# Softmax sums of an attention: ones-matmul on TensorE, or a trip through DRAM

## The chip, the cores and the metric

One core of a Trainium2 chip runs the whole kernel in one launch. TensorE multiplies matrices, VectorE and ScalarE work on SBUF and PSUM, GpSimd does little here, and SyncE (SP) issues nearly all DMAs. Times are device microseconds. The time before is the median of three runs; the profile is of one further execution with its own time.

## The reference

The input is x of shape (4, 256, 64, 64) in fp32: four images of 256 channels and 4096 pixels. Four layers follow, each of the form x = x + layer(group_norm(x)). The change lies in the first, whose middle is an attention over all pixels:

```python
xs = relu(group_norm(conv3x3(x, smooth_w) + smooth_b))
f = einsum('bnc,bcm->bnm', theta_x, phi_x)      # 4096 x 4096 logits per image, 128 channels
attn = softmax(f, axis=-1)
y = einsum('bnm,bmc->bnc', attn, g_x)
w_y = group_norm(conv1x1(y, w_w, w_b))
return w_y * 0.1 + xs
```

The other three layers are a linear attention, a convolution with generated filters and a mix of expert matrices. All is fp32.

## The kernel before, in words

**The attention.** `attend(b)` is a generator over one image. It takes the 4096 queries in eight blocks of 512 (`NQ = 8`), and each block in 16 steps of 256 keys (`NM = 16`). Keys stand on partitions, queries along the free dimension. In a step, `logits(i + 1)` makes the next step's two tiles pf of 128 keys by 512 queries (L984) and ScalarE exponentiates them into pr (L985). Then two matmuls add g times pr to the block's output py in PSUM (L1040), and VectorE adds pr to tot, a tile of 128 x 1024 running sums (L124, a helper's line). There is no maximum to subtract.

**The end of a block.** After step 15, tot holds for each query sums that are still spread over 128 partitions and two halves. `ended` finishes them: VectorE adds the two halves into inv (L992) and leaves a check sum in guard; a matmul with a matrix of ones (L996) sums over the partitions and leaves the total of each query on every partition (pss); VectorE inverts it (L1013, 128 x 512 elements); yt = py * inv; ScalarE runs through inv once for the second check sum (L1017); two matmuls with ww give ps_wy (L1021), copied to wt (L1022). wt gets statistics (L1025) and goes to DRAM as wy_d. In the last image also the residual's block xc is loaded from xs_d and its statistics are taken (L1051, L963). `ended` is itself a generator, kept in `todo`: it goes on by one `yield` at the end of each step of the next block, after that step's addition to tot.

**The order of the work.** The order on every engine is that of the program, written out by hand (`manual_schedule`). While image b attends, a `Chain` puts other work between its steps: the rest of the previous image's layers (`tail`) and the convolution of the next image (`convolve`, `convolve_second`, with filter tiles u loaded ahead at L478). `run` advances the attention by a step per unit of the chain. An engine executes its list in order, and each instruction waits for semaphores. So an instruction that waits holds up all behind it on its engine. SP too works through its DMAs in one order: a DMA that waits for another's landing, or for VectorE, holds up the next ones' issue.

**Buffers.** `k4` is a pool of nine tiles of 128 x 1024 (pr, tot, wt, xc and the chain's tiles), `k2` one of five tiles of 128 x 512 (yt, parts of products, res, the tiles of the output). PSUM has eight banks, one pool. inv has one buffer.

Of the kernel before, what the change touches and what calls it, by code (L numbers as in the profile page):

```python
# [8 lines left out]
F32 = mybir.dt.float32  # L9
AF = mybir.ActivationFunctionType  # L10
ALU = mybir.AluOpType
AX = mybir.AxisListType

P = 128
NH = 2
HW = 64
N = HW * HW
CH = 1024
# [6 lines left out]
NQ = N // 512  # L25
# [68 lines left out]
def conv_preact_fast(ctx: ExitStack, tc: tile.TileContext, guard, x, wc, wtpg, ww, wqkv, wout, w1cat, wd2,  # L94
# [3 lines left out]
    nc = tc.nc  # L98
    B = x.shape[0]

    cp = ctx.enter_context(tc.tile_pool(name="const", bufs=1))
    wk = ctx.enter_context(tc.tile_pool(name="work", bufs=1))
    sp = ctx.enter_context(tc.tile_pool(name="small", bufs=2))
    pp = ctx.enter_context(tc.tile_pool(name="ps", bufs=1, space=bass.MemoryType.PSUM))

    def k4(name):
        return wk.tile([P, CH], F32, tag="k4", name=name, bufs=9)
# [1 line left out]
    pool4 = k4  # L109

    def k2(name):
        return wk.tile([P, 512], F32, tag="k2", name=name, bufs=5)

    def filter_tile(name):
        return wk.tile([P, NH, NH * P], F32, tag="u", name=name, bufs=3)
# [1 line left out]
    def junk():  # L117
        return wk.tile([P, 512], F32, tag="junk", name="junk")

    def bank(name):  # L120
        return pp.tile([P, 512], F32, tag="bank", name=name, bufs=8)

    def tt(o, a, b, op):
        nc.vector.tensor_tensor(o, a, b, op)  # L124
# [33 lines left out]
    def resident(name, src):  # L158
        t = cp.tile(list(src.shape), F32, name=name)
        nc.sync.dma_start(out=t, in_=src)  # L160
        return t
# [8 lines left out]
    ww_s = resident("ww_s", ww)  # L170
# [50 lines left out]
    def scale_weights(w):  # L221


        nc.vector.tensor_scalar(bo_s, bo_s, 1.0 / HEADS, None, ALU.mult)

        nc.vector.tensor_scalar(gains, vec_s[:, V_GN:V_GN + 2, :], float(NH * P) ** 0.5, None, ALU.mult)
        for h in range(NH):
            nc.vector.tensor_scalar(wqkv_s[:, h, :], wqkv_s[:, h, :], gains[:, 0, h:h + 1], None, ALU.mult)
        yield 1.5

        ps = bank("ps_wn")
        for h in range(NH):
            sq = k2("wsq")
            nc.scalar.activation(sq[:, 0:2 * HID], wqkv_s[:, h, 0:2 * HID], AF.Square)
            yield 1
            nc.tensor.matmul(ps[:, 0:2 * HID], ones, sq[:, 0:2 * HID], start=(h == 0), stop=(h == NH - 1))
        wmax = sp.tile([P, 1], F32, name="wmax", bufs=1)
        nc.vector.tensor_reduce(wmax, ps[:, 0:2 * HID], AX.X, ALU.max)
        for side in range(2):
            nc.vector.tensor_scalar(guard[:, side, B * NQ:B * NQ + 1], wmax, GUARD_MAX[side] / NORM2_MAX, None, ALU.mult)  # L240
# [157 lines left out]
    xs_d = tc.dram_tile([B, NH, P, N], F32, name="xs_d")  # L398
    wy_d = tc.dram_tile([B, NH, P, N], F32, name="wy_d")
# [536 lines left out]
    NM = N // CH * 4  # L936

    wy_stats = {}


    res_st = cp.tile([P, NH, NQ, 6], F32, name="res_st")
# [7 lines left out]
    def residual_known():  # L949
        nc.vector.tensor_scalar(factors[:, 0, :], vec_s[:, V_G2W, :], 0.1, None, ALU.mult)  # L950
        nc.vector.tensor_scalar(factors[:, 1, :], vec_s[:, V_G2B, :], 0.1, None, ALU.mult)
        res_mv.append(sp.tile([P, NH, 2], F32, name="rmv", bufs=1))
        for h in range(NH):
            nc.vector.bn_aggr(res_mv[0][:, h, :], res_st[:, h, :, :].rearrange("p c s -> p (c s)"))
        tt(res_shift, res_mv[0][:, :, 0], factors[:, 1, :], ALU.add)

    def attend(b):

        probs, todo = {}, []
        st = wy_stats[b] = sp.tile([P, NH, 8, 6], F32, name="wy_st")  # L960

        def multiply(q, h, wt, xc):
            nc.vector.scalar_tensor_tensor(xc[:, h, :], wt[:, h, :], pivot_in[:, h:h + 1], xc[:, h, :], ALU.add, ALU.mult,  # L963
                                           accum_out=joint[:, h, q:q + 1])

        def with_residual(q, wt, xc):

            if q == 0:
                mv = sp.tile([P, NH, 2], F32, name="mv")
                for h in range(NH):  # L970
                    nc.vector.bn_aggr(mv[:, h, :], st[:, h, 0, :])
                nc.vector.tensor_scalar(pivot_in, mv[:, :, 0], -1.0, None, ALU.mult)
            if q < NQ - 1:
                for h in range(NH):
                    multiply(q, h, wt, xc)
            else:
                last_block.extend(lambda h=h: multiply(q, h, wt, xc) for h in range(NH))

        def logits(i):
            q, m = divmod(i, NM)  # L980
            pr = k4("pr")
            for s in range(2):
                pf = bank("pf")
                nc.tensor.matmul(pf, phi[:, bass.ts(2 * m + s, P)], theta[:, bass.ts(q, 512)], start=True, stop=True)  # L984
                nc.scalar.activation(pr[:, bass.ts(s, 512)], pf, AF.Exp)  # L985
            probs[i] = pr

        def ended(q, py, tot, xc):

            at = b * NQ + q  # L990
            inv = wk.tile([P, 512], F32, tag="inv", name="inv")
            nc.vector.scalar_tensor_tensor(inv, tot[:, 0:512], 1.0, tot[:, 512:CH], ALU.mult, ALU.add,  # L992
                                           accum_out=guard[:, 0, at:at + 1])
            yield
            pss = bank("pss")
            nc.tensor.matmul(pss, ones, inv, start=True, stop=True)  # L996
            wt = k4("wt").rearrange("p (h n) -> p h n", h=NH)
            if at == B * NQ - 1:

                yt = k2("yt")  # L1000
                nc.scalar.copy(yt, py)
                banks = [bank("ps_wy") for _ in range(NH)]
                for h in range(NH):
                    nc.tensor.matmul(banks[h], ww_s[:, bass.ts(h, P)], yt, start=True, stop=True)
                yield
                nc.vector.reciprocal(inv, pss)
                for h in range(NH):
                    tt(wt[:, h, :], banks[h], inv, ALU.mult)
                nc.scalar.activation(junk(), inv, AF.Copy, accum_out=guard[:, 1, at:at + 1])
                yield  # L1010
            else:
                yield
                nc.vector.reciprocal(inv, pss)  # L1013
                yt = k2("yt")
                tt(yt, py, inv, ALU.mult)
                yield
                nc.scalar.activation(junk(), inv, AF.Copy, accum_out=guard[:, 1, at:at + 1])  # L1017

                for h in range(NH):
                    ps = bank("ps_wy")  # L1020
                    nc.tensor.matmul(ps, ww_s[:, bass.ts(h, P)], yt, start=True, stop=True)  # L1021
                    nc.scalar.copy(wt[:, h, :], ps)  # L1022
            yield
            for h in range(NH):
                nc.vector.bn_stats(st[:, h, q, :], wt[:, h, :])  # L1025
            nc.sync.dma_start(out=wy_d[b].rearrange("h p n -> p h n")[:, :, bass.ts(q, 512)], in_=wt)
            if b == B - 1:
                with_residual(q, wt, xc)

        xc = None  # L1030
        logits(0)
        for i in range(NQ * NM):
            q, m = divmod(i, NM)
            if m == 0:
                py = bank("py")
                tot = k4("tot")
            if i + 1 < NQ * NM:
                logits(i + 1)
            for s in range(2):
                nc.tensor.matmul(py, g[:, bass.ts(2 * m + s, P)], probs[i][:, bass.ts(s, 512)],  # L1040
                                 start=(m == 0 and s == 0), stop=(m == NM - 1 and s == 1))
            if m == 1:
                tt(tot, probs[i - 1], probs[i], ALU.add)
            elif m > 1:
                tt(tot, tot, probs[i], ALU.add)
            if b == B - 1 and m == 9:
                xc = k4("xc").rearrange("p (h n) -> p h n", h=NH)
                nc.sync.dma_start(out=xc, in_=xs_d[b].rearrange("h p n -> p h n")[:, :, bass.ts(q, 512)])
            if b == B - 1 and m in (12, 14):
                h = m // 2 - 6  # L1050
                nc.vector.bn_stats(res_st[:, h, q, :], xc[:, h, :])  # L1051
                if q == NQ - 1 and h == NH - 1:
                    residual_known()
            for t in todo:
                next(t, None)
            if m == NM - 1:
                todo = [ended(q, py, tot, xc)]
                next(todo[0])
            yield i + 1 < NQ * NM
        for t in todo:  # L1060
            for _ in t:
                yield
# [1284 lines left out]
```

## Time and profile before

| | |
|---|---|
| median of three runs | 3085.98 us (3084.27 to 3086.03) |
| the profiled execution | 3084.23 us |
| its span | 3082.4 us |
| TensorE busy, instructions | 3000.3 us (97%), 8606 |
| VectorE busy | 2128.5 us (69%) |
| ScalarE busy | 1162.0 us (38%) |
| DMA, mean rate | 178.45 MB, 58 GB/s |
| TensorE's granted clock | 0.993 |

A row of a profile gives the line and engine, what is written from what, the shape and the count; then the busy time, the mean of one in ns, and the idle time of the engine just before, with the one that ended it. PE is matmul, PEld the load of a matmul's weights, which overlaps the matmuls; DVE is VectorE, ACT ScalarE, SPq SyncE's queue. Ends of matmuls are modelled, so their starts tell more than their durations. The attention of image 0 runs from 185 to 757 us, of image 1 to 1501, of image 2 to 2242 and of image 3 to about 2820; the last image's remaining layers follow alone.

### The profile page before, as it was taken

Reading aid. Unit: us, or ns where it says so; the run is one execution under the profiler, and the core shown is the slowest. Engines: PE = TensorE matmul, PEld = TensorE weight load, DVE = VectorE, ACT = ScalarE, POOL = GpSimd, SP = SyncE. Lnnn points to the kernel's source line nnn. Section 1 sums busy time; section 2 is a strip of 40 time slices with the busy share of each in tenths; the row PEclk is TensorE's granted clock in tenths of the full one; section 3 lists DMA queues with packets and bytes.
Section 4 is the critical chain, followed back from the end, with each engine's and each line's share of the span. In section 5 each row is a group of like instructions: output and inputs, shape, how many; then the busy total and the mean of one; then the engine's idle time right before and its main releaser. Section 6 shows DMA issues by size and latency. Waiting matters only on the chain.

```text
span 3082.4 us, 24468 instructions
## 1 busy us (share of the span) xinstructions
PE 3000.3 (97%) x8606; PEld 1483.7 (48%) x8606; DVE 2128.5 (69%) x2780; ACT 1162.0 (38%) x2155; POOL 132.1 (4%) x178
## 2 busy tenths in 40 slices
PE   6899999999999999999999999999999999999998
PEld 3454555445554444444565444444546544444643
DVE  8747777853547996777536797678563569876485
ACT  2334333353555332223364532222436453334621
POOL 0100000000010000000011000000001100000100
PEclk9999999999999999999999999999999999999999
DMA  5233111122100023113300102311420000022021
GB/s 219 84 101 137 34 48 32 34 52 73 57 11 28 14 75 122 39 40 66 116 1 11 35 7 82 123 45 38 96 82 14 18 28 28 14 82 89 8 69 66
DMA packets 61089, 178.45 MB, mean 58 GB/s; under 512 B 6560, under 2 KB 16544, under 8 KB 56736
## 3 DMA queue, kind: packets, MB, share of 16 engines
q1 hardware_dynamic: 56928, 160.04, 15.1%
q0 software_dynamic: 4032, 16.78, 2.9%
q8 instruction: 70, 1.15, 0.2%
q14 instruction: 59, 0.48, 0.1%
HBM read 115.45 MB, written 78.12 MB: 63 GB/s over the span
## 4 chain that ended last, share of the span: by engine, by line
PE 77%; DVE 16%; issue 5%; ACT 1%; POOL 0%; DMA 0%; POOLq 0%; DVEq 0%; ACTq 0%
PE pf L984 22%; PE py L1040 22%; PE ps_qkv L1201 5%; PE ps_conv L512 4%; PE ps_tp L926 4%; DVE dw L127 4%; PE ps_ex L1660 4%; DVE tot L124 3%; PE ps_pw L1460 3%; PE ps_conv L584 2%; PE ps_g L931 2%; PE ps_wy L1021 2%; PE ps_o L1287 1%; PE ps_dw L1505 1%; DVE big L127 1%
## 5 line engine op out<-in xcount | busy, mean ns | idle before, releaser
L985 ACT ACTIVATE pr<-pf 128x512 f32<-128x512 f32 x1024 | 603.9, 597 | 1195.4 <-PE pf L984 1147.9
L984 PE MATMUL pf<-tpg 128*128 128x512 f32 x2048 | 968.9, 595 | 2.9 <-ACT pr L985 2.9
L1040 PE MATMUL py<-pr,tpg 128*128 128x512 f32 x2048 | 962.3, 592 | 2.5 <-ACT pr L985 2.3
L124 DVE TENSOR_TENSOR tot<-tot,pr 128x1024 f32<-128x1024 f32 x448 | 546.3, 1219 | 174.1 <-ACT pr L985 172.5
L1040 PEld LDWEIGHTS py<-pr,tpg 128*128 128x128 f32 x2048 | 388.6, 190 | 494.6 <-issue 477.6
L984 PEld LDWEIGHTS pf<-tpg 128*128 128x128 f32 x2048 | 382.0, 190 | 438.4 <-issue 412.6
L127 DVE SCALAR_TENSOR_TENSOR dw<-xp,dk,dw 128x1008 f32<-128x1008 f32 x208 | 263.0, 1268 | 9.9 <-ACT dw L1452 7.0
L512 PE MATMUL ps_conv<-v,u 128*128 128x512 f32 x384 | 171.0, 593 | 3.6 <-DVE v L124 3.6
L1201 PE MATMUL ps_qkv<-wqkv_s,xg 128*128 128x384 f32 x384 | 129.9, 487 | 0.0
L124 DVE TENSOR_TENSOR tpg<-ps_g,bg_s 128x512 f32<-128x512 f32 x32 | 22.1, 692 | 145.2 <-PE ps_g L931 145.2
L926 PE MATMUL ps_tp<-big,wtpg_s 128*128 128x512 f32 x256 | 117.7, 603 | 3.0 <-ACT big L684 3.0
L512 PEld LDWEIGHTS ps_conv<-v,u 128*128 128x128 f32 x384 | 72.6, 190 | 96.5 <-issue 89.8
L217 POOL TENSOR_TENSOR rstd<-rstd,half 128x2 f32<-128x2 f32 x24 | 17.6, 731 | 2342.1 <-DVE rstd L365 2225.2
L1013 DVE RECIPROCAL inv<-pss 128x512 f32<-128x512 f32 x31 | 103.9, 3352 | 5.5 <-PE pss L996 5.5
L1460 PE MATMUL ps_pw<-dw,pk 128*128 128x512 f32 x224 | 101.3, 592 | 0.0
L1201 PEld LDWEIGHTS ps_qkv<-wqkv_s,xg 128*128 128x128 f32 x384 | 72.2, 190 | 53.6 <-issue 9.8
L1220 DVE TENSOR_REDUCE qs<-qk 128x16 f32<-128x512 f32 x24 | 16.5, 686 | 117.4 <-ACT qk L1214 117.4
L927 ACT ACTIVATE tpg<-ps_tp,btp_s 128x512 f32<-128x512 f32 x64 | 43.8, 687 | 119.2 <-PE ps_tp L926 119.2
L926 PEld LDWEIGHTS ps_tp<-big,wtpg_s 128*128 128x128 f32 x256 | 47.8, 194 | 54.9 <-issue 50.4
L1289 ACT ACTIVATE junk<-ps_o 128x256 f32<-128x256 f32 x128 | 49.2, 385 | 63.9 <-PE ps_o L1287 56.3
L1214 ACT ACTIVATE qk<-ps_qkv,rinv 128x256 f32<-128x256 f32 x96 | 45.6, 475 | 72.4 <-PE ps_qkv L1201 60.0
L124 DVE TENSOR_TENSOR v<-ra 128x1024 f32<-128x1024 f32 x58 | 69.5, 1220 | 0.4
(369 smaller groups left out, 3132.7 us busy)
## 6 DMA issues: line engine op xcount, KB each, us to landing
xp<-in_x_dram SPq DMA_DIRECT2D x16, 1024.0 KB, 6.3
wy_d<-wt SPq DMA_DIRECT2D x32, 512.0 KB, 3.0
wy<-wy_d SPq DMA_DIRECT2D x32, 512.0 KB, 4.9
out_dram<-res SPq DMA_DIRECT2D x64, 256.0 KB, 2.0
xs_d<-big POOLq DMA_DIRECT2D x24, 512.0 KB, 11.1
u<-filters SPq DMA_DIRECT2D x48, 256.0 KB, 2.5
xs<-xs_d SPq DMA_DIRECT2D x24, 512.0 KB, 6.1
u<-rows_d SPq DMA_DIRECT2D x36, 256.0 KB, 3.1
```

The costliest lines, as they stand in the source:

```text
L124: nc.vector.tensor_tensor(o, a, b, op)
L127: nc.vector.scalar_tensor_tensor(o, a, s, b, op0, op1)
L512: nc.tensor.matmul(ps[oh], u(oh, h), v[:, bass.ts(h, 512)], start=(h == 0), stop=(h == NH - 1))
L584: nc.tensor.matmul(ps[:, bass.ts(oh, IY * IX)], u[i][:, h, bass.ts(oh, P)], v[:, i, bass.ts(h, IY * IX)], start=(h == 0), stop=(h == NH - 1))
L926: nc.tensor.matmul(ps, wtpg_s[:, h, k, :], big[:, h, cols], start=(h == 0), stop=(h == NH - 1))
L984: nc.tensor.matmul(pf, phi[:, bass.ts(2 * m + s, P)], theta[:, bass.ts(q, 512)], start=True, stop=True)
L985: nc.scalar.activation(pr[:, bass.ts(s, 512)], pf, AF.Exp)
L1013: nc.vector.reciprocal(inv, pss)
L1040: nc.tensor.matmul(py, g[:, bass.ts(2 * m + s, P)], probs[i][:, bass.ts(s, 512)], start=(m == 0 and s == 0), stop=(m == NM - 1 and s == 1))
L1201: nc.tensor.matmul(ps[:, 0:3 * HID], xg[:, h, bass.ts(j, P)], wqkv_s[:, h, :], start=(h == 0), stop=(h == NH - 1))
L1460: nc.tensor.matmul(ps, pk[:, h * NH * P + oh * P:h * NH * P + (oh + 1) * P], dw[h][:, bass.ts(s, 512)], start=(h == 0), stop=(h == NH - 1))
L1660: nc.tensor.matmul(ps, wm[h][:, bass.ts(oh, P)], big[:, h, bass.ts(c, 512)], start=(h == 0), stop=(h == NH - 1))
```

## The change

For the first seven blocks of each image, 28 of 32, `ended_by_dram` replaces `ended`; the eighth block goes as before. py is copied to SBUF at once. The halves' sums inv (128 partitions x 512 queries) are stored to DRAM, and loaded back so that partition r holds, for four queries 4r to 4r + 3, the 128 parts of each: 128 x 4 floats along the free dimension, in pieces of four. VectorE sums over the parts, inverts 128 x 4 values, and they are stored (2 KB) and loaded again with every partition getting all 512. Then yq = yq * inv, the two ww matmuls, and the rest. Each DMA stands some `yield`s, that is steps of the next block, ahead of what uses it. The residual's block xc of the last image is loaded and measured inside `ended_by_dram` for these blocks. k2 gets four tiles in place of five, and a tile yq is new.

```diff
-        return wk.tile([P, 512], F32, tag="k2", name=name, bufs=5)
+        return wk.tile([P, 512], F32, tag="k2", name=name, bufs=4)
...
+    sum_d = tc.dram_tile([B * NQ, P, 512], F32, name="sum_d")
+    rec_d = tc.dram_tile([B * NQ, 512], F32, name="rec_d")
...
+        def residual_block(q):
+            t = k4("xc").rearrange("p (h n) -> p h n", h=NH)
+            nc.sync.dma_start(out=t, in_=xs_d[b].rearrange("h p n -> p h n")[:, :, bass.ts(q, 512)])
+            return t
...
+        def projected(q, wt, xc):
+            for h in range(NH):
+                nc.vector.bn_stats(st[:, h, q, :], wt[:, h, :])
+            nc.sync.dma_start(out=wy_d[b].rearrange("h p n -> p h n")[:, :, bass.ts(q, 512)], in_=wt)
+            if b == B - 1:
+                with_residual(q, wt, xc)
+
+        def ended_by_dram(q, py, tot):
+            at = b * NQ + q
+            inv = wk.tile([P, 512], F32, tag="inv", name="inv")
+            nc.vector.scalar_tensor_tensor(inv, tot[:, 0:512], 1.0, tot[:, 512:CH], ALU.mult, ALU.add,
+                                           accum_out=guard[:, 0, at:at + 1])
+            yt = wk.tile([P, 512], F32, tag="yq", name="yq")
+            nc.scalar.copy(yt, py)
+            nc.sync.dma_start(out=sum_d[at], in_=inv)
+            yield
+            yield
+            nc.sync.dma_start(out=inv.rearrange("r (p k) -> r p k", k=4), in_=sum_d[at].rearrange("p (r k) -> r p k", k=4))
+            yield
+            yield
+            yield
+            r = sp.tile([P, 4], F32, name="r_inv", bufs=1)
+            nc.vector.tensor_reduce(r, inv.rearrange("r (p k) -> r k p", k=4), AX.X, ALU.add)
+            nc.vector.reciprocal(r, r)
+            nc.vector.tensor_reduce(guard[:, 1, at:at + 1], r, AX.X, ALU.add)
+            nc.sync.dma_start(out=rec_d[at].rearrange("(r k) -> r k", k=4), in_=r)
+            xc = residual_block(q) if b == B - 1 else None
+            yield
+            yield
+            nc.sync.dma_start(out=inv, in_=rec_d[at].partition_broadcast(P))
+            yield
+            yield
+            tt(yt, yt, inv, ALU.mult)
+            yield
+            wt = k4("wt").rearrange("p (h n) -> p h n", h=NH)
+            for h in range(NH):
+                ps = bank("ps_wy")
+                nc.tensor.matmul(ps, ww_s[:, bass.ts(h, P)], yt, start=True, stop=True)
+                nc.scalar.copy(wt[:, h, :], ps)
+            if b == B - 1:
+                for h in range(NH):
+                    residual_stats(q, h, xc)
+            yield
+            projected(q, wt, xc)
...
-            if b == B - 1 and m == 9:
...
+            if b == B - 1 and q == NQ - 1 and m == 9:
+                xc = residual_block(q)
...
-                todo = [ended(q, py, tot, xc)]
+                todo = [ended_by_dram(q, py, tot) if q < NQ - 1 else ended(q, py, tot, xc)]
```

## The prediction

> **What bounds the kernel now.** I read the page's busy times first, then the chain, then single instructions at a block's end, then the Vector engine's order and the DMA queues there.
>
> The busy times of the page:
>
> ```profile
> span 3082.4 us, 24468 instructions
> ...
> PE 3000.3 (97%) x8606; PEld 1483.7 (48%) x8606; DVE 2128.5 (69%) x2780; ACT 1162.0 (38%) x2155; POOL 132.1 (4%) x178
> ```
>
> TensorE is busy 97% of the span, but its ends are modelled, so that alone proves little. The chain that ended last agrees:
>
> ```profile
> PE 77%; DVE 16%; issue 5%; ACT 1%; POOL 0%; DMA 0%; POOLq 0%; DVEq 0%; ACTq 0%
> ```
>
> Three quarters of the end time is matmuls that follow one another; DMA is nothing. Now the timeline at the end of image 0's first query block (start, duration, engine, line):
>
> ```profile
> 245.40 0.19 PEld L996 LDWEIGHTS pss<-inv,ones 128*128 128x128 f32 x1 [0.24 <-issue]
> 245.82 1.02 PE L996 MATMUL pss<-inv,ones 128*128 128x512 f32 x2
> 245.82 0.19 PEld L996 LDWEIGHTS pss<-inv,ones 128*128 128x128 f32 x1 [0.24 <-issue]
> 246.25 0.19 PEld L984 LDWEIGHTS pf<-tpg 128*128 128x128 f32 x1 [0.24 <-issue]
> 246.88 3.36 DVE L1013 RECIPROCAL inv<-pss 128x512 f32<-128x512 f32 x1 [0.68 <-PE pss L996]
> ```
>
> The weight loads stand 0.43 us apart: that is what one fp32 instruction of 512 columns costs the stream, not the 0.59 us of its row. One matmul in the code is two of these, 0.86 us. The sum over 128 partitions fits in the same rhythm: it costs 0.86 us per block and nothing waits around it. Since the starts leave hardly any gap in the attention stages, any 0.43 us taken out of TensorE there is time.
>
> The tile view of the sums, minimum/median/maximum in ns:
>
> ```profile
> L996 PE MATMUL pss<-inv,ones x64: 592/592/1061, 245.8 to 2818.2; 128*128 128x512 f32 x64
> L1013 DVE RECIPROCAL inv<-pss x31: 3342/3351/3358, 246.9 to 2766.7; 128x512 f32<-128x512 f32 x31
> ```
>
> 64 instructions are 32 blocks of two; 28 blocks change.
>
> [...] The load that regroups the sums has pieces of four floats, 16 bytes, so 128 x 128 = 16384 of them, 1024 on each of 16 DMA engines. No DMA of the kernel before is like it. [...]
>
> **The change part by part**, for one block.
>
> TensorE: minus one ones-matmul, 2 x 0.43 = 0.86 us. The two ps_wy matmuls only move from the second to the ninth step after the block. 28 x 0.86 = 24.0 us less.
>
> VectorE: minus 3.35 (reciprocal) and 0.69 (yt from PSUM). Plus the reduction to four sums: the nearest row is TENSOR_REDUCE 128x16<-128x512 at 0.69; [...] I take 0.69. Plus a reciprocal and a sum of four elements, 0.16 each by the small rows (L1629, L1625), plus yq times inverse, 0.69. Net 4.04 - 1.70 = 2.3 us less, 65 us in all, on an engine 69% busy: hidden by TensorE, worth nothing by itself except as slack.
>
> ScalarE: minus the junk copy with its accumulator, 0.62 + 0.19; plus a copy of py, 0.59 (row L1001). It sits between the exponentials of two steps, where that engine idles about 2 us for pf. No cost; if chain work filled the gap, 0.59 us a block. The py bank comes free sooner and the pss bank is not taken.
>
> Buffers: k2 has four tiles in place of five, but yt no longer uses them. The result tiles, beside wm, have three. One is held for 0.69 (add) + 0.4 (issue) + 2.0 (landing), about 3.3 us with waits; a piece of output comes every 4 x 0.43 = 1.7 us, so three suffice. Only the fourth of the first four back-to-back adds waits, about 1.5 us, three times over the kernel; most is covered by banks. I take 1 us in all.
>
> DMA and waits: four DMAs per block, all on SP. Store of the sums (256 KB): the output stores of that size land in 2.0, so 3 us after the sums with issue and semaphores. Then the gather, time T. Then VectorE's reduction stands waiting in line for it, with everything of VectorE behind it: the next additions to tot, which free the pr tiles for ScalarE, and the next convolution rows or dw terms, which TensorE's other work needs. Then a 2 KB store of inverses (2.0 us), the broadcast load of 256 KB (the 128 KB one of bo took 3.3, so about 4 us), used four steps after the reduction: four steps of at least 3.43 us are 13.7, against 0.7 + 0.4 + 2.1 + 0.4 + 4 = 7.6. Hidden. On SP the 2 KB store waits for VectorE, with filter loads behind it in places; these are issued 8.4 to 24 us before their first matmul and land in 2.5 to 3.1.
>
> T decides. The nearest thing is the start, where small loads (64 to 576 bytes a piece) drain. DMA queues from 20.7 to 20.9 us:
>
> ```profile
> DMA packets 140, 0.01 MB, mean 71 GB/s; under 512 B 131, under 2 KB 140, under 8 KB 140
> q1 hardware_dynamic: 140, 0.01, 54.1%
> ```
>
> The share gives 0.541 x 16 x 0.2 / 140 = 12.4 ns of an engine per packet: 1024 x 12.4 = 12.7 us, with 2.1 fixed (what a 1 KB load took) 14.8. The pace, 140 in 0.2 us, gives 16384 / 0.7 per ns = 23.4, so 25.5. [...] I take 17.
>
> How long may T be? The reduction stands after the fourth addition to tot of the next block. VectorE's timeline where this comes soonest, image 0, second block:
>
> ```profile
> 298.77 0.69 DVE L992 SCALAR_TENSOR_TENSOR inv<-tot 128x512 f32<-128x512 f32 x1
> ...
> 302.89 1.23 DVE L124 TENSOR_TENSOR tot<-pr 128x1024 f32<-128x1024 f32 x1 [0.89 <-ACT pr L985]
> ...
> 310.04 1.22 DVE L124 TENSOR_TENSOR tot<-tot,pr 128x1024 f32<-128x1024 f32 x1
> ...
> 312.38 1.22 DVE L124 TENSOR_TENSOR tot<-tot,pr 128x1024 f32<-128x1024 f32 x1
> ...
> 315.90 1.22 DVE L124 TENSOR_TENSOR tot<-tot,pr 128x1024 f32<-128x1024 f32 x1
> ```
>
> From 299.5 to 317.1 is a lead of 17.6 us. It cannot shrink much when the reciprocal goes, as five steps of TensorE are 17.2. The leads of the 28 blocks, read in the same way: image 0 21, 18, 23, 28, 22, 19, 18; images 1 and 2 47, 23, 26, 24, 27, 32, 40; image 3 36, 31, 24, 20, 22, 27, 25. The DMA engines are nearly idle in these leads (from 299 to 315 almost no packet), so the gather meets little traffic. A stall is T + 3.5 - lead. About 3.5 us of it is absorbed (my estimate: one step of spare pr tiles and banks), so the loss is the sum of T - lead where positive. T = 17: nothing. Filter loads caught behind it come at most 12 us late against leads of 18 to 24 there.
>
> Sum against the profiled execution of 3084.2 (span 3082.4 and 1.8 around it): 3084.2 - 24.0 + 1 = 3061.2. The median of the runs is 1.8 above that execution, so 3063.
>
> **Rivals.**
>
> Slower: the gather is the new bound. Place: VectorE at the reduction. With T = 30 the shortfalls from the leads add up to 61 us in image 0, 20 in each of images 1 and 2, 32 in image 3: 133 - 24 = +109, 3195. T = 50 would give some +600. It decides from T = 24 (loss 33, net +9). For it: 16384 pieces is far beyond any DMA of this trace, whose small ones have at most 16 per engine and were already queued, so their drain says nothing of making them. Against: even that partial pace of 0.7 per ns gives only 25.
>
> No change: the wait eats the gain. T of 22 to 24, a loss of 15 to 33 us mainly in image 0 and image 3's middle blocks; or filter loads of image 0 with 8.4 us in hand get caught behind the gather; 3086. For: those leads of 18 to 20. Against: it is a narrow band.
>
> More than forecast: VectorE's 65 us also shortens the chain's 16% on that engine. All of TensorE's gaps after 185 us are under 60 us, most of them in the last image after the attention; a tenth gives 3057.
>
> That the matmul isn't removed is excluded: the changed order has 28 fewer on TensorE.
>
> **Numbers.** Forecast 0.50, more than it 0.05, no change 0.10, slower 0.35. A measurement here can tell about 0.2%, 6 us. So faster 0.55, same 0.10, slower 0.35. The low end is the larger gain with some margin, 3050; the high end takes in T up to 30, 3200, and leaves out the tail above, some 0.18. The forecast's own range is 3054 to 3078.
>
> **What would show it.** Right: TensorE's matmul count down by 56; a gather landing 10 to 20 us after issue; r_inv's reduction idle before it under 20 us in total; weight loads still 0.43 us apart at block ends. Wrong: a large idle time of VectorE released by DMA inv<-sum_d, TensorE's stalls on pr or tot behind it, and a DMA share near one for tens of us after each block.

## The result

| | before | after |
|---|---|---|
| median of eight runs each | 3086.14 us | 3075.86 us (3071.98 to 3076.67) |
| ratio | | 0.9968, 95% interval 0.9959 to 0.9976 |
| the profiled execution, its span | 3084.23, 3082.4 us | 3076.46, 3073.7 us |

The kernel became 10.3 us faster, where 23 us were forecast. The sign and the price of the matmuls were right; more than half of the gain was lost elsewhere. The page of the changed kernel, its busy times, its DMA packets and its chain:

```profile
span 3073.7 us, 24553 instructions
...
PE 2980.7 (97%) x8550; PEld 1475.7 (48%) x8550; DVE 2071.8 (67%) x2836; ACT 1160.1 (38%) x2127; POOL 131.8 (4%) x178
...
DMA packets 532387, 200.55 MB, mean 65 GB/s; under 512 B 470688, under 2 KB 480672, under 8 KB 528032
...
PE 70%; DVE 8%; issue 1%; ACT 1%; POOL 0%; DMA 0%; DVEq 0%; POOLq 0%; ACTq 0%
```

TensorE has 56 matmul instructions fewer and is still 97% busy. The kernel before had 61089 packets; the change adds 16832 for each of its 28 blocks, 16384 of them those of the gather, as the load that regroups the sums is called from here on. The DMA share of the chain is still 0%, so the loss isn't to be seen there. The tile view of inv shows what VectorE waited for (minimum/median/maximum in ns, then idle us and times):

```profile
L1025 DVE TENSOR_REDUCE r_inv<-inv x28: 1049/1068/1180, 258.4 to 2768.5; 128x4 f32<-128x512 f32 x28
...
  DMA inv<-sum_d: 39.6, 6
  DMA inv<-rec_d: 14.9, 5
```

And the DMA view of the changed kernel (the last number is the median from issue to landing, us):

```profile
sum_d<-inv SPq DMA_DIRECT2D x28, 256.0 KB, 2.0
inv<-sum_d SPq DMA_DIRECT2D x28, 256.0 KB, 11.4
inv<-rec_d SPq DMA_DIRECT2D x28, 256.0 KB, 4.2
```

The gather takes 11.4 us, well under the 17 that were taken. Yet VectorE waits 39.6 us for it in six of 28 blocks. So the median tells nothing of six blocks. They are the first six of image 0, where the gather was issued 2.6 to 18.2 us after the sums; in the others VectorE's wait for it is 0.1 us or none. To see what that costs, the span is cut at the first logits of each image (us; the last part is what follows the last logits):

| kernel | head | image 0 | image 1 | image 2 | image 3 | tail |
|---|---|---|---|---|---|---|
| before | 184.9 | 572.8 | 743.3 | 741.5 | 571.5 | 268.4 |
| changed | 186.0 | 575.5 | 739.4 | 736.1 | 565.5 | 271.3 |

The forecast was 7 x 0.86 = 6.0 us less in every image. Image 3 gives exactly 6.0. Image 2 gives 5.4, image 1 gives 3.9, and image 0 became 2.7 us longer; the tail costs 2.9 and the head 1.1.

In image 0, the second block is the costliest place. VectorE, then TensorE, in the timelines of the changed kernel (start, duration, and in brackets the idle time before, with what ended it):

```profile
326.01 1.05 DVE L1025 TENSOR_REDUCE r_inv<-inv 128x4 f32<-128x512 f32 x1 [11.30 <-DMA inv<-sum_d]
```

```profile
319.52 1.88 PE L1096 MATMUL py<-pr,tpg 128*128 128x512 f32 x4
328.12 6.69 PE L584 MATMUL ps_conv<-v,u 128*128 128x256 f32 x16 [6.72 <-DVE v L124]
```

VectorE stands 11.3 us before the reduction, and TensorE 6.7 us behind it. And more is lost after it. The same place in stretches of 4 us (busy time of PE, PEld, DVE, ACT, POOL, then the granted clock, DMA share and GB/s):

```profile
322.00:326.00 4.00, 0.00 (x0) 0.00 (x0) 0.00 (x0) 0.00 (x0) 0.00 (x0) 0.74 1.12 76
326.00:330.00 4.00, 1.89 (x5) 1.53 (x6) 3.81 (x6) 0.00 (x0) 0.00 (x0) 0.50 0.01 3
330.00:334.00 4.00, 4.00 (x11) 3.19 (x10) 1.23 (x1) 0.60 (x1) 0.00 (x0) 0.50 0.22 65
```

For 4 us no engine works at all; only DMAs run. Within them, at 323.9, TensorE's clock is halved, for 10.2 us. It is idle for the first 4.2 of them; the 6.0 from 328.1 to 334.1 run at a granted clock of 0.50 and cost, by estimate, half of that, 3.0 us. 6.7 + 3.0 = 9.7 us in this one block. In the traces before and changed, every half-clock period after 185 us lasts 3.4, 6.8 or 10.2 us, apart from the last, which reaches past the last instruction, and all these changes of the clock lie, within a trace, on one grid of 3.41 us, to 0.02. In the window of the grid just ahead of this period, from 320.5 to 323.9, TensorE was still busy for 0.88 us: its last matmul ends, by the profile's model, at 321.4, 2.5 us before the clock is halved.

Why was this gather late? SyncE's queue, first before, then changed:

```profile
256.08 0.38 SPq L1026 DMA_DIRECT2D wy_d<-wt  x1
256.50 2.51 SPq L478 DMA_DIRECT2D u<-filters  x2
259.05 1.20 SPq L661 DMA_DIRECT2D xs_d<-in_x_dram  x2
```

```profile
280.40 0.37 SPq L1004 DMA_DIRECT2D wy_d<-wt  x1
299.76 0.33 SPq L1017 DMA_DIRECT2D sum_d<-inv  x1
300.14 0.93 SPq L478 DMA_DIRECT2D u<-filters  x2
301.11 1.13 SPq L661 DMA_DIRECT2D xs_d<-in_x_dram  x2
302.34 0.54 SPq L1020 DMA_DIRECT2D inv<-sum_d  x1
```

Before, SP issued the first filter loads and the copy of x (4 MB from DRAM to DRAM) at 256 to 260 us, and had no other DMA to issue until 314. In the changed kernel wy_d comes 24 us later, as its wt does, and then the new store stands in SP's order ahead of the filter loads and the copy. The store waits for the second block's sums, until 299.8. So filters and copy go out at 300, immediately before the gather. Its first packets move 15.2 us after the sums. That the DMA engines were idle from 299 to 315 in the kernel before (a DMA share of 0.00, 1 GB/s) was the work of an SP that ran ahead of the other engines, and the change takes that away.

### The profile page after: what moved, and what is told of

It is laid out like the page before. It is cut to its first block, busy times and chain, and to the rows that moved or that the text cites. A ratio compares the mean times of both kernels' runs of the same rounds, so it can differ in the third digit from the quotient of the medians.

```text
span 3073.7 us, 24553 instructions
## 1 busy us (share of the span) xinstructions
PE 2980.7 (97%) x8550; PEld 1475.7 (48%) x8550; DVE 2071.8 (67%) x2836; ACT 1160.1 (38%) x2127; POOL 131.8 (4%) x178
## 4 chain that ended last, share of the span: by engine, by line
PE 70%; DVE 8%; issue 1%; ACT 1%; POOL 0%; DMA 0%; DVEq 0%; POOLq 0%; ACTq 0%
PE pf L986 21%; PE py L1096 20%; PE ps_qkv L1253 5%; PE ps_conv L512 4%; PE ps_pw L1512 4%; PE ps_ex L1712 3%; PE ps_tp L926 3%; PE ps_o L1339 2%; PE ps_g L931 1%; DVE big L127 1%; PE ps_wy L1040 1%; DVE tot L124 1%; PE ps_ctx L1284 1%; PE ps_ss L1244 1%; PE ps_dw L1557 1%
## 5 line engine op out<-in xcount | busy, mean ns | idle before, releaser
L584 PE MATMUL ps_conv<-v,u 128*128 128x256 f32 x288 | 68.4, 392 | 10.0 <-DVE v L124 10.0
```

The costliest lines, as they stand in the source:

```text
L584: nc.tensor.matmul(ps[:, bass.ts(oh, IY * IX)], u[i][:, h, bass.ts(oh, P)], v[:, i, bass.ts(h, IY * IX)], start=(h == 0), stop=(h == NH - 1))
```

## The experiments

The letters of the theories are those of the expectations. In short: theory A and its kin put the missing time into image 0's gathers that come late, the others into what every image pays. The theory of SP's order (S) came last, from SP's queues before and changed.

**The trip to DRAM left out.** All four DMAs of a block are gone, so the denominators of the first seven blocks are not computed; every other instruction stays.

```diff
-            nc.sync.dma_start(out=sum_d[at], in_=inv)
...
-            nc.sync.dma_start(out=inv.rearrange(...), in_=sum_d[at].rearrange(...))
...
-            nc.sync.dma_start(out=rec_d[at].rearrange("(r k) -> r k", k=4), in_=r)
...
-            nc.sync.dma_start(out=inv, in_=rec_d[at].partition_broadcast(P))
```

> The changed kernel without its four DMAs of the sums per block: the reduction reads the unsent halves' sums of its own partition and yq is multiplied by them, so the softmax denominators of the first seven blocks are left out of the computation; every instruction of VectorE, ScalarE and TensorE stays. It prices the removed matmuls alone. Theory A: TensorE's 24.0 us less and no wait, plus what the buffers cost: 3062 to 3065. Rival B, in the form that VectorE's or ScalarE's changed order costs time and not the DMAs: 3070 or more.

Measured 3061.34 us, 0.9923 (0.9910 to 0.9937) of before, 22.9 us less. Image 0 took 561.7, images 1 and 2 739.3 and 736.1, image 3 565.5, the tail 271.1. Image 3's 6.0 us less bear out the price of the matmuls. That the total does too is partly luck: image 0 gained 11.1 us, which makes up for what images 1 and 2 and the tail lack. In its sixth block, more went with the ones-matmul than its own time. In the kernel before, TensorE once waited there for VectorE's sums:

```profile
588.81 1.65 PE L996 MATMUL pss<-inv,ones 128*128 128x512 f32 x2 [3.03 <-DVE inv L992]
```

The 3.4 us of half clock from 589.3 that followed were worth, by estimate, up to half of that, 1.7 more. Both are gone here and in the changed kernel, where TensorE no longer needs the sums: 6.0 + 3.0 + 1.7 = 10.7.

Of the 14.5 us between this kernel and the changed one, 13.8 lie in image 0. But images 1 and 2 and the tail are as in the changed kernel: what is missing there has nothing to do with the DMAs.

**Image 0 the old way.**

```diff
-                todo = [ended_by_dram(q, py, tot) if q < NQ - 1 else ended(q, py, tot, xc)]
+                todo = [ended_by_dram(q, py, tot) if q < NQ - 1 and b > 0 else ended(q, py, tot, xc)]
```

> Image 0's blocks end the old way (ones-matmul, reciprocal on 128 x 512), images 1 to 3 as changed: 21 blocks change. Theory A (all of the loss but some 5 us lies in image 0): faster than the changed kernel by some 3 us, 3073. Rival B (the loss is spread over the 28 blocks, so each nets 0.37 us): slower than the changed kernel by 2.6, 3078.5.

Measured 3068.88 us (3068.58 to 3073.05), 0.9950 (0.9937 to 0.9964). With the change in three images alone the kernel is 7 us faster than with it in four: theory A's sign, and 4 us more than it asked for. Image 0 took 572.8 as before, image 1 736.2, that is 3 us less than in the changed kernel.

Those 3 us are the clock. At the end of image 1 TensorE waits for VectorE's statistics mv, 3.04 us in both kernels (1.32 in the kernel before). The changed kernel there, and then this one, in the same columns as above:

```profile
1427.00:1431.00 4.00, 0.96 (x4) 0.69 (x4) 3.97 (x9) 0.67 (x2) 0.00 (x0) 0.85 0.34 131
1431.00:1435.00 4.00, 4.00 (x5) 1.58 (x6) 3.28 (x8) 1.04 (x2) 0.00 (x0) 0.50 0.00 0
```

```profile
1424.00:1428.00 4.00, 0.96 (x4) 0.52 (x4) 3.96 (x9) 0.62 (x2) 0.00 (x0) 1.00 0.34 131
1428.00:1432.00 4.00, 4.00 (x12) 1.93 (x11) 3.38 (x9) 1.19 (x2) 0.36 (x1) 1.00 0.00 0
```

The same wait and the same work beside it; 5 matmuls in the 4 us that follow against 12. The one wait was followed by 6.8 us of half clock, the other by none. What differs is where the wait falls on the grid of 3.41 us. One window of the grid in the changed kernel, then two in this one:

```profile
1426.42:1429.84 3.42, 0.85 (x2) 0.02 (x1) 3.42 (x8) 1.17 (x2) 0.00 (x0) 1.00 0.30 116
```

```profile
1422.46:1425.87 3.41, 1.76 (x5) 0.45 (x3) 3.41 (x7) 1.17 (x2) 0.00 (x0) 1.00 0.03 13
1425.87:1429.28 3.41, 2.02 (x6) 1.09 (x7) 3.27 (x11) 0.60 (x1) 0.00 (x0) 1.00 0.37 141
```

In the changed kernel most of the wait lies in one window and leaves TensorE busy for 0.85 us of it; here two windows share it. In all fourteen traces after 185 us, the windows at full clock in which TensorE was busy for less than 40% are 72, and half clock followed each; of the 99 between 40 and 60% it followed 22, and of the 11506 above 60% none. In the traces before and changed alone these are 9 of 9, 3 of 12 and none of 1650. So the wait of 3.04 us had 6.8 us of half clock behind it where most of it fell into one window, and none where two shared it.

**The gather directly behind the store.**

```diff
             nc.sync.dma_start(out=sum_d[at], in_=inv)
+            nc.sync.dma_start(out=inv.rearrange(...), in_=sum_d[at].rearrange(...))
             yield
             yield
-            nc.sync.dma_start(out=inv.rearrange(...), in_=sum_d[at].rearrange(...))
             yield
```

> The gather of the sums follows its store directly in SP's order (five steps ahead of the reduction instead of three); all else is the changed kernel's. Theory A (in image 0 the gather came late: it stood on SP behind filter loads that wait for TensorE, and in the DMA rings behind the copy of x): its issue moves to about 2 us after the sums in every block, VectorE's wait for it (39.6 us in the changed kernel) goes to under 5, image 0 shortens by 8 to 9 us, time about 3067. Rival B (the trip costs something in every block, wherever the gather stands): the wait goes, the time stays within 3 us of 3076.

Measured 3067.11 us (3066.04 to 3067.46), 0.9941 (0.9928 to 0.9955). Image 0 took 565.5, 10.0 less than changed: in the second block the gather now stands ahead of filters and copy. Theory A's time came, its wait of under 5 us did not: VectorE still waits 13.7 us in two later blocks, where the store itself stands behind filter loads and goes out 15.0 and 5.4 us after the sums.

**The changed kernel once more, and with the copy of x two products later.** The first has no edit. The second:

```diff
         us = load_filters(0)
-        copy_x(1)
         for i, (a, pair) in enumerate(PRODUCTS):
+            if i == 2:
+                copy_x(1)
```

> The changed kernel again, beside the others on one chip: 0.9968 of the kernel before, as measured first.

> The changed kernel with the copy of image 1 into xs_d, 4 MB from DRAM to DRAM, issued two products later in the chain of image 0, so that it no longer stands ahead of the second block's gather in the DMA rings. Theory A1 (the copy is what held that gather up): the 11.3 us of VectorE there go, with TensorE's 6.7 us and the half clock behind it; image 0 shortens by 7 to 9, about 3068. Theory A2 (SP's order behind filter loads is most of it): 3074 or more, since blocks three to six of image 0 keep their late gathers.

Measured 3076.09 us for the changed kernel, which repeats it with all its parts within 0.9 us, and 3066.83 us (3063.47 to 3067.59), 0.9939 (0.9925 to 0.9952), with the copy moved. Image 0 took 565.7. The gather's place in SP's order is as in the changed kernel, and only the copy has left it. The waits of VectorE in this kernel (us in all, times, the longest):

```profile
DVE r_inv L1026 <- DMA inv<-sum_d: 28.6, 5, 9.3
```

Waits of 4.8 to 9.3 us are still there in four blocks of image 0. Against the 561.7 without any trip they cost 4.0 us at most. So the copy ahead of one gather was the 10 us, and what the filter loads ahead of the other stores and gathers cause is mostly absorbed.

**The store on another queue.** ScalarE issues the store of the sums, and SP's order is free of it.

```diff
-            nc.sync.dma_start(out=sum_d[at], in_=inv)
+            nc.scalar.dma_start(out=sum_d[at], in_=inv)
```

> The changed kernel with one DMA per block on another queue: ScalarE issues the store of the sums, in place of SP. Nothing else moves. Theory S (the store is what did the harm: on SP it stands ahead of the first filter loads and the copy of x in image 0, waits there for the second block's sums, and so holds these from 256 to 259 us, where the kernel before issues them, until 300 us, in front of the gather): with the store gone from SP's order, SP issues filters and copy directly behind wy_d, at 281 us, 20 us before the gather; the second block's gather lands within 12 us of its issue, VectorE waits there under 1 us, TensorE has no half clock after 185 us in image 0, and image 0 takes 565.6 us; total 3066 us. Rival (the copy and the filter loads meet the gather wherever they are, or what was lost there is the filter loads' and not the copy's): image 0 stays at 575. Second rival (ScalarE, which now waits some 1 to 2 us for VectorE's sums before its next exponentials, delays TensorE by more than its slack): image 3, which has nothing else to lose, takes over 567 us in place of 565.5, and 28 such delays of 0.5 us add 14 us.

Measured 3069.06 us (3067.97 to 3070.0), 0.9947 (0.9933 to 0.9960). SP's queue in this kernel:

```profile
280.00 1.34 SPq L478 DMA_DIRECT2D u<-filters  x2
281.80 1.14 SPq L661 DMA_DIRECT2D xs_d<-in_x_dram  x2
303.92 0.38 SPq L1020 DMA_DIRECT2D inv<-sum_d  x1
```

Filters and copy go out at 280 to 283, behind wy_d, as theory S said, with nothing moved in the program but the store's queue. The second block's reduction starts 16.4 us after the sums, VectorE idles 1.4 us ahead of it, and TensorE doesn't stall there. So it is the store's wait in SP's order that put the copy ahead of the gather. In the other blocks the gather is as late as before; VectorE's waits for it are 26.7 us in all.

Image 0 took 568.7, not 565.6, and there the second rival has a point. ScalarE's longest wait for the sums, and TensorE behind it:

```profile
ACT pr L987 <- DVE inv L1013: 12.2, 3, 8.4
```

```profile
588.04 3.78 PE L1096 MATMUL py<-pr,tpg 128*128 128x512 f32 x4 [4.50 <-ACT pr L987]
```

ScalarE, which now issues the store, stands for 8.4 us until the sums are there, and its exponentials come late: TensorE stalls 4.5 us, with 6.8 us of half clock from 585.7. It is the sixth block, where TensorE itself waited for the sums in the kernel before. The change had taken that wait away, and the store on ScalarE brings it back by another engine. Image 3 stayed at 565.5, so ScalarE's shorter waits cost nothing there.

**Store and gather on ScalarE.**

```diff
-            nc.sync.dma_start(out=sum_d[at], in_=inv)
+            nc.scalar.dma_start(out=sum_d[at], in_=inv)
+            nc.scalar.dma_start(out=inv.rearrange(...), in_=sum_d[at].rearrange(...))
             yield
             yield
-            nc.sync.dma_start(out=inv.rearrange(...), in_=sum_d[at].rearrange(...))
```

> The changed kernel with the store of the sums and the gather, directly behind it, both issued by ScalarE, so that neither ever stands behind a filter load on SP. Theory S: the gather is issued 2 us after the store in every block, VectorE's waits for inv<-sum_d fall from 39.6 us to under 5, and image 0 comes near the 561.7 us that it takes without any trip; total 3062 to 3064 us, if ScalarE's wait of about 2 us for the store's landing costs nothing. Rival: ScalarE stands some 3.5 us in each of 28 blocks with full pf banks behind it, TensorE has one step of 1.7 us in hand and stalls for up to 1.8 us each time: up to 50 us, image 3 at 578, total 3080 to 3110 us.

Measured 3074.39 us (3073.8 to 3075.91), 0.9965 (0.9951 to 0.9978): neither the 3064 of the one nor the 3080 of the other. VectorE's waits for the gather are down to 2.1 us or less in each block. In its place:

```profile
ACT pr L987 <- DMA sum_d<-inv: 32.2, 10, 10.5
```

ScalarE's exponentials now wait 32.2 us, up to 10.5 at once. The view puts this down to the store's landing, which came last; of the 10.5 us, some 8 are the wait for the sixth block's sums again, which are there at 588.3, and 2 the landing. TensorE stalls 6.6 us behind it, and 6.8 us of half clock follow from 589.6. Image 0 took 571.9 and image 3 566.1. The wait has moved to an engine with less slack.

**Pieces of eight bytes.** The gather directly behind the store, as two DMAs, each of half of every piece: 32768 pieces in place of 16384 for the same bytes.

```diff
             nc.sync.dma_start(out=sum_d[at], in_=inv)
+            for a in range(2):
+                nc.sync.dma_start(out=inv.rearrange(...)[:, :, 2 * a:2 * a + 2], in_=sum_d[at].rearrange(...)[:, :, 2 * a:2 * a + 2])
             yield
             yield
-            nc.sync.dma_start(out=inv.rearrange(...), in_=sum_d[at].rearrange(...))
```

> The gather first, but in two DMAs that each take every other pair of floats: 8-byte pieces, twice as many, the same bytes. If the time of the gather goes by pieces: 20 to 21 us from issue to landing in place of 11.4, so it lands 22.5 us after the sums; by the leads of the prediction the shortfalls beyond 3.5 us add up to some 20 us of time, 3087. If it goes by bytes: 11 to 13 us, and 3067 to 3069.

Measured 3172.23 us (3171.41 to 3173.73), 1.0281 (1.0265 to 1.0297). Where VectorE waits in images 1 to 3, the reduction starts 22.9 to 23.8 us after the sums, with the first issue at 2.1: some 21 us for both. With 2.1 us fixed, as in the prediction, an estimate is (11.4 - 2.1) / 1024 = 9.1 ns for each piece of an engine with sixteen bytes, and (21 - 2.1) / 2048 = 9.2 ns with eight. Bytes are equal and pieces doubled, and the time went from 11.4 us to some 21, with the pieces. The landing came as expected, the 3087 did not: the kernel lost 105 us against its neighbour with one gather. The two differ in more than pieces, as SP is held for 9.2 us by the issue of the two gathers and what stands behind it comes late. Its waits:

```profile
DVE r_inv L1027 <- DMA inv<-sum_d: 108.6, 17, 18.9
PE ps_conv L512 <- DMA u<-rows_d: 37.1, 4, 11.1
```

**Four k2 tiles in the kernel before, and the kernel before once more.** The first is the kernel before with bufs=4 in place of 5 for k2; the second has no edit.

> The kernel before with four k2 buffers instead of five, nothing else. If the fifth buffer accounts for the 2.9 us that the last image's remaining layers lost after the attention: 3089. If not (the prediction took 1 us): 3086 to 3087.

> The kernel before once more, for a second trace of its part after the last logits, which took 268.4 us in the first trace and 270.3 to 271.8 in every trace of a kernel with the change or with four k2 tiles. If k2 or the change cost those 2 to 3 us there, it is again 268.4 within 0.5 us, and the head again 184.9. If the part differs by itself from execution to execution (where the half-clock periods fall), it may be anything from 268.4 to 271.8.

Four tiles: 3086.74 us (3085.91 to 3087.86), 1.0006 (0.9998 to 1.0014), which tells nothing apart; its tail is 270.4. The kernel before repeated: 3084.92 in its one run, with images 0 to 3 within 0.05 us of the first trace, and a tail of 269.1 against 268.4, which speaks for neither theory.

**A shared pool, and everything together.** The gather first, and yq taken from a k2 of five tiles; then the same with the copy later as well.

```diff
-        return wk.tile([P, 512], F32, tag="k2", name=name, bufs=4)
+        return wk.tile([P, 512], F32, tag="k2", name=name, bufs=5)
...
-            yt = wk.tile([P, 512], F32, tag="yq", name="yq")
+            yt = k2("yq")
```

> The kernel with the gather directly after its store, and five k2 tiles with yq taken from them in place of four and one of its own (the same memory). The last image's remaining layers then have five k2 tiles again: if the fourth tile's loss there is real, about 2 us less than with the gather first alone, 3065; if not, the same 3067.

> The changed kernel with three edits together: the gather issued directly after the store, yq taken from a k2 of five tiles, and the copy of x issued two products later. Theory A (the lost time of image 0 is one stall of TensorE behind a gather that queued behind the copy of x, with the half clock after it; either edit alone removes it): the edits do not add, since both remove the same stall: image 0 again 565.6 us from first to last, total 3066 us, within 2 us of either edit alone. Rival C (each edit also removes waits of its own that the other leaves): some 3 to 5 us below the single edits, 3061 to 3063 us.

Measured 3065.58 us (3064.25 to 3066.07), 0.9937 (0.9923 to 0.9950), the lowest median of the variants that compute everything; and 3066.67 (3062.37 to 3067.85), 0.9940 (0.9926 to 0.9953), for all three edits. Theory A of the second expectation holds: the two edits remove one and the same stall and don't add. Which of the variants between 3065.6 and 3067.1 is best can't be told; the last had 6.8 us of half clock at the end of image 2, where the others have 3.4 or none, and 738.7 us there in place of 736 to 737.

Their tails say more on the question of k2. The instructions after the last logits are the same in both, with five k2 tiles in both, and take 270.9 in the one and 268.4 in the other. The first has two periods of half clock in the middle of the tail, of 6.8 and 3.4 us, the second only one of 6.8; 1.7 of the 2.5 us arise at the second period. So a tail of 271 needs no fourth tile to explain it. Whether four tiles cost anything besides stays open: all traces with four lie between 270.3 and 271.9.

## Why the prediction was right and wrong

**TensorE, 24.0 us less: right as the price of the matmuls.** Image 3 gave 6.0 of 6.0. That without the trip the kernel gained 22.9 of the 23.0 that the sum had is partly luck, since image 0's 11.1 cover what is missing elsewhere. That "nothing waits around it" held in the block that was read, but not in the sixth of image 0, where TensorE waited 3.0 us for the sums. The rival of a larger gain came near this; it put most of TensorE's gaps in the last image after the attention, where about half are, 21 of 43 us.

**VectorE, 2.3 us less a block, worth nothing: nearly.** It is 56.7 us less busy, 2.0 a block. The reduction took 1.07 and not 0.69, 55% more than the row it was taken from, which differs in stride and in the number of outputs.

**The gather's time T of 17: right in what follows, too high.** It took 11.4, the median of 28. The trace has 16384 packets for a gather, as many as it has pieces. The 17 was the author's estimate, between the 14.8 and the 25.5 read from the packets that drain at the start; what was measured lies below both. By estimate from the runs a piece took 9.1 ns of an engine, against 12.4 in the row of draining packets.

**The broadcast, "Hidden": not in image 0.** It landed in 4.2 us as priced, but five blocks of image 0 come to it late, and VectorE waits 14.9 us for it. With the copy later these waits are 15.1 us, and are part of what costs 4.0 at most.

**The step that failed.** "The DMA engines are nearly idle in these leads (from 299 to 315 almost no packet), so the gather meets little traffic." This read the traffic of the kernel before at the gather's place, where SP had issued the copy 40 us ahead. The prediction asked what is queued behind the store of the inverses, which waits for VectorE; it didn't ask it of the store of the sums, which waits for VectorE as well. Behind that stood the copy and the filter loads. SP's order is fixed in the program, and so are the new waits in it: that the store of the second block precedes copy and filters, and that the filter loads ahead of the gathers of later blocks wait for TensorE, could be read before any run. With "3 us after the sums" as the gather's start, what was measured in image 0 is 2.1 to 18.2 us. In the second block the issue came in time, at 2.6, and the traffic did the harm: behind the copy the gather landed 23.6 us after its issue, where 17 were taken and 11.4 is the median, and this cost 9.8 us.

**The leads, and "3.5 us of it is absorbed".** In image 0 up to 9.3 us of VectorE's wait was absorbed nearly whole, where the copy stayed away, so 3.5 was too small for a single wait; the same model was too mild on many: with 21 us for a gather its sum of T - lead gives 9 us of loss, and the pieces of eight bytes lost 105. The rest of that loss lies in things it left out, filter loads that come late and half clock (clock 0.979 over the run). "It decides from T = 24" is therefore too late.

**The rest of the missing gain.** The sum asked for 23.0 us less of span, and 8.7 came. Of the 14.3 missing, the second block of image 0 is 9.8 (575.5 - 565.7). The waits that remain in image 0 with the copy later are 4.0 at most (565.7 - 561.7). Images 1 and 2 lack 2.1 and 0.6, which they lack without the trip too; longer waits for statistics with half clock behind them are there, and account for 3 us in image 1. The tail costs 1.9 more than the 1 us allowed, and the head 1.1. The last item is the other sign: without any trip image 0 gains 5.1 more than 6.0 (572.8 - 561.7 - 6.0), as the wait for the sums and the half clock at 589 are gone there. Together 9.8 + 4.0 + 2.7 + 1.9 + 1.1 - 5.1 = 14.4, within rounding. The tail is shown to vary by 2.5 us between two kernels that run the same instructions in it, most of that with the clock; the head's 1.1 has no cause shown, and heads of all traces lie between 184.4 and 186.8.

**The signs.** The matmul count and the landing time were as announced for the right case, and VectorE's idle time of 39.6 us by the gather as announced for the wrong one. Both were true: the forecast treated 28 blocks as one, and one of them carried most of the loss.

## What to carry to other kernels

Before a DMA that waits is put on a queue, list what stands behind it in that queue's order, and when the kernel before issued it: a quiet stretch of the DMA engines may be quiet only because their queue ran ahead. A price by the median of many equal steps doesn't see the one step that meets something else. Another queue is no free way out: the store on ScalarE's queue freed SP's order and held ScalarE's own work until the sums were there, up to 8.4 us. And one wait of TensorE of 3.04 us had 6.8 us of half clock behind it in one kernel and none in another, as it fell differently on the grid of 3.41 us: two kernels with the same wait differ there by 3 us.

## What the hardware showed

- A gather of 16384 pieces of 16 bytes took 11.4 us (the median of 28 in the changed kernel), by estimate 9.1 ns a piece on each of 16 engines; with pieces of 8 bytes the same estimate gave 9.2.
- DMAs that SP issued right behind such a gather took long to issue. With the gather directly behind its store, a filter load behind the second block's gather took 8.9 us to issue; in the changed kernel, behind the gather that stood behind the copy, it took 21.4 us, until 1.6 us before that gather landed. The gather's own issue took 0.37 us as the median. In the kernel with pieces of eight bytes, two gathers in a row:

```profile
303.31 9.23 SPq L1019 DMA_DIRECT2D inv<-sum_d  x2
```

- A reduction over a stride of 16 bytes took 1.07 us for 512 columns, against 0.69 for a reduction of the same size in the kernel before.
- Half clock, a granted clock of 0.50, came in periods of 3.4, 6.8 and 10.2 us. In the fourteen traces it followed all 72 windows of 3.41 us at full clock in which TensorE was busy for less than 40%, and none of the 11506 in which it was busy for more than 60%. The same wait of 3.04 us was followed by 6.8 us of it in the changed kernel and by none with image 0 the old way; after the last logits of the kernel before it also came, for 6.8 us from 2828.4, where the longest single wait was 1.5 us.
